# The last output block of the down projection moved into the else part of a runtime branch, with its last tile cut in two

## The chip, the cores and the metric

The kernel runs on one core of one Trainium2 chip. Times are device microseconds of one execution. The time shown for a kernel is the median of several executions; a separate execution is recorded by the hardware profiler, and that one has its own time and its own span (from the first to the last instruction of the program).

## The reference

For 2048 tokens (8 batches of 256) of 1024 features: each batch picks one of eight adapters of rank 16, and the feed-forward part works on the adapter's output, with activations rounded to FP8. The result is added to x.

```python
c      = (x @ B[adapter].T) @ A[adapter].T        # rank 16, per batch of 256 tokens
gate   = fp8(c / gate_in_scale) @ (gate_w * scales).T    # 1024 -> 2752
up     = fp8(c / up_in_scale)   @ (up_w * scales).T      # 1024 -> 2752
hidden = silu(gate) * up
out    = x + fp8(hidden / down_in_scale) @ (down_w * scales).T   # 2752 -> 1024
```

The weights are given as float32 that already hold FP8 values. `fp8` clips to 448 and rounds to float8_e4m3fn.

## The kernel before

Everything is kept transposed: features lie on the 128 partitions, tokens along the free dimension. `NH = 8` blocks of 128 features, `NI = 22` blocks of the hidden size (21 full ones and a tail of 64 rows), `NTB = 4` blocks of `TB = 512` tokens.

**Fast path.** After the adapters, `gate_up(c, t)` (L523) makes hidden block c for token block t: 16 matmuls of 128x128 weights by 512 tokens, a Silu on ScalarE (L553) and a product on VectorE that rounds to FP8 (L554). The down projection is the loop over k (L642 to L674), one k for each of the eight output blocks. For one k there are four PSUM tiles `yd`, one for each t; each takes 21 matmuls (L658) and one matmul of the 64-row tail (`tail_of`, L623). The tail of an even k is multiplied together with that of the next k, in one group of eight matmuls (L626), since two half-height matmuls run side by side. `finish` (L634) scales a tile and adds x on VectorE (L636), and starts its store from SyncE (L639); its output tile `o` has three buffers.

**The check.** The fast path takes the upper 16 bits of each float32 weight, and the chip's own FP8. That is exact only if the lower bits are zero and no rounded value reaches a limit. ScalarE therefore sums the low bits of every weight tile (`note_low_bits`, L408) and the squares of every rounded tile (`note_squares`, L415). `outside` (L604) reduces these sums with four VectorE instructions to one number for each partition, adds them over the partitions with one float32 matmul (L617), turns the sum into an integer (L619) and has every engine load it into a register (L620). It is called inside k = 7, before the last token block. If the number is positive, `general` (L67) computes everything again in three parts of each weight and with its own rounding, and overwrites the output. With this input it is never entered: the engines jump over it (L676).

**What sets the order.** A scheduler places the instructions on each engine; those wrapped in `keep_in_program_order` stay where the program has them (all of `multiply`, L423). Each engine runs its own list in order, and waits on semaphores. All weight loads and all stores of the output are issued by SyncE in one order (one queue), and the five weight buffers of the pool `w` come free when the matmuls and the low-bit sums have read them. [...]

Of the kernel before, what the change touches and what calls it, by code (L numbers as in the profile page):

```python
# [18 lines left out]
P = 128  # L19
# [47 lines left out]
def general(  # L67
# [20 lines left out]
    wpool = ctx.enter_context(tc.tile_pool(name="g_w", bufs=1))  # L88
    work = ctx.enter_context(tc.tile_pool(name="g_work", bufs=2))
    xg = acts.tile([P, NH, T], BF16, name="g_xg")  # L90
    xu = acts.tile([P, NH, T], BF16, name="g_xu")
    hid = acts.tile([P, NI, T], BF16, name="g_hid")
# [48 lines left out]
    with tc.tile_pool(name="g_lora", bufs=1) as lora:  # L141
        b_sb = lora.tile([P, NH, P], F32, name="g_b")
        nc.sync.dma_start(out=b_sb, in_=bT)
        a_sb = lora.tile([P, H], F32, name="g_a")
        nc.scalar.dma_start(out=a_sb, in_=aT)
        for t in range(NTB):
            cols = bass.ts(t, TB)
            bx = psum.tile([P, TB], F32, tag="ps", name="g_bx")
            for k in range(NH):
                xk = lora.tile([P, TB], F32, tag="xk", name="g_xk", bufs=2)  # L150
                nc.sync.dma_start(out=xk, in_=x4[t][:, k, :])
                nc.tensor.matmul(
                    bx, lhsT=b_sb[:, k, :], rhs=xk, start=(k == 0), stop=(k == NH - 1)
                )
            bm = lora.tile([P, TB], F32, tag="bm", name="g_bm")
            for j in range(TB // SEQ):
                b = t * (TB // SEQ) + j
                nc.vector.tensor_scalar(
                    bm[:, bass.ts(j, SEQ)],
                    bx[:, bass.ts(j, SEQ)],  # L160
                    mask[:, b : b + 1],
                    None,
                    ALU.mult,
                )
            for k in range(NH):
                c = psum.tile([P, TB], F32, tag="ps", name="g_c")
                nc.tensor.matmul(
                    c, lhsT=a_sb[:, bass.ts(k, P)], rhs=bm, start=True, stop=True
                )
                for to, s in ((xg, GATE_IN), (xu, UP_IN)):  # L170
                    v = work.tile([P, TB], F32, tag="v", name="g_v")
                    nc.scalar.activation(v, c, AF.Copy, scale=inv[:, s : s + 1])
                    quantize(to[:, k, cols], v, P)

    for c in range(NI):
        n = rows_of(c)
        w = wpool.tile([P, 2 * NH * P], F32, tag="w", name="g_wgu")
        at = c * 2 * NH * P
        nc.sync.dma_start(out=w[:, : 2 * NH * n], in_=w_gu[:, at : at + 2 * NH * n])
        w = w[:, : 2 * NH * n]  # L180

        order = "p (j k n) -> p j k n" if n == P else "p (k j n) -> p j k n"
        ws = [
            high(part).rearrange(order, j=2, k=NH) for part in three_parts(w)
        ]
        for t in range(NTB):
            cols = bass.ts(t, TB)
            ps = []
            for j, x in enumerate((xg, xu)):
                y = psum.tile([P, TB], F32, tag="ps", name=f"g_y{j}")[:n]  # L190
                terms = [(k, part) for part in ws for k in range(NH)]
                for i, (k, part) in enumerate(terms):
                    nc.tensor.matmul(
                        y,
                        lhsT=part[:, j, k, :],
                        rhs=x[:, k, cols],
                        start=(i == 0),
                        stop=(i == len(terms) - 1),
                    )
                ps.append(y)  # L200
# [11 lines left out]
            quantize(hid[:n, c, cols], v, n)  # L212

    for k in range(NH):
        ys = [psum.tile([P, TB], F32, tag="ps", name=f"g_yd{t}") for t in range(NTB)]
        for half in range(2):
            first = half * HALF
            full = HALF - half
            w = wpool.tile([P, 2 * NH * P], F32, tag="w", name="g_wd")
            w = w[:, : HALF * P].rearrange("p (c n) -> p c n", n=P)  # L220
            nc.sync.dma_start(out=w[:, :full], in_=w_d[k][:, first : first + full, :])
            if half:
                nc.sync.dma_start(out=w[:TAIL, full], in_=w_d_tail[:, k, :])
            terms = [(part, i) for part in three_parts(w[:, :full]) for i in range(full)]
            for t in range(NTB):
                for i, (part, at) in enumerate(terms):
                    nc.tensor.matmul(
                        ys[t],
                        lhsT=high(part[:, at, :]),
                        rhs=hid[:, first + at, bass.ts(t, TB)],  # L230
                        start=(half == 0 and i == 0),
                        stop=False,
                    )
        tail = three_parts(w[:TAIL, HALF - 1])
        for t in range(NTB):
            cols = bass.ts(t, TB)
            for i, part in enumerate(tail):
                nc.tensor.matmul(
                    ys[t],
                    lhsT=high(part),  # L240
                    rhs=hid[:TAIL, NI - 1, cols],
# [7 lines left out]
                o, in0=ys[t], scalar=down_s, in1=xr, op0=ALU.mult, op1=ALU.add  # L249
            )  # L250
            nc.gpsimd.dma_start(out=outT[bass.ts(k, P), cols], in_=o)
# [3 lines left out]
def adaln_ffn(  # L255
# [24 lines left out]
    nc.vector.memset(zeros, 0.0)  # L280

# [7 lines left out]

    with ExitStack() as fast:  # L290
        acts = fast.enter_context(tc.tile_pool(name="acts", bufs=1))
        lora = fast.enter_context(tc.tile_pool(name="lora", bufs=1))
        wpool = fast.enter_context(tc.tile_pool(name="w", bufs=5))
# [4 lines left out]
        xg = [acts.tile([P, NH, TB], FP8, name=f"xg{t}") for t in range(NTB)]  # L298
        hid = [acts.tile([P, T], FP8, name=f"hid{c}") for c in range(NI - 1)]


        hid_tail = acts.tile([P, 2, TB], BF16, name="hid_tail")
# [96 lines left out]


        wt = acts.tile([P, NH, P], F32, name="w_dt")
# [202 lines left out]
        def outside():  # L604

            nc.vector.tensor_scalar(ok[:, :NLOW], lows, 0.0, None, ALU.is_le)
            nc.vector.tensor_scalar(
                ok[:, NLOW : NLOW + NSQ], squares, SAME_MAX**2, None, ALU.is_lt
            )
            least = const.tile([P, 1], F32, name="least")  # L610
            nc.vector.tensor_reduce(least, ok, AX.X, ALU.min)
            found = const.tile([P, 1], F32, name="found")
            nc.vector.tensor_scalar(found, least, 0.5, None, ALU.is_lt)
            ones = const.tile([P, 1], F32, name="ones")
            nc.vector.memset(ones, 1.0)
            count = psum.tile([P, TB], F32, tag="ps", name="count")
            nc.tensor.matmul(count[:1, :1], lhsT=found, rhs=ones, start=True, stop=True)  # L617
            count_i = const.tile([1, 1], I32, name="count_i")
            nc.vector.tensor_copy(count_i, count[:1, :1])  # L619
            return nc.values_load(count_i[0:1, 0:1], min_val=0, max_val=P)  # L620


        def tail_of(k, ys, start):  # L623

            for t in range(NTB):
                nc.tensor.matmul(  # L626
                    ys[t],
                    lhsT=high(wt[half_of(t), k, :]),
                    rhs=hid_tail[half_of(t), t // 2],
# [4 lines left out]
        def finish(k, t, y):  # L634
            o = work.tile([P, TB], F32, tag="o", name="o")
            nc.vector.scalar_tensor_tensor(  # L636
                o, in0=y, scalar=down_s, in1=xs[t][:, k, :], op0=ALU.mult, op1=ALU.add
            )
            nc.sync.dma_start(out=outT[bass.ts(k, P), bass.ts(t, TB)], in_=o)  # L639


        for k in range(NH):  # L642
            ws = []
            for half in range(2):
# [4 lines left out]
                ws += [w[:, i, :] for i in range(n)]  # L649
            if k == 0:  # L650
                note_squares(hid_tail, P, NSQ - 1)
                note_low_bits(wt, P, NLOW - 1)
            first = k % 2 == 0
            if first:
                ys = [psum.tile([P, TB], F32, tag="ps", name=f"yd{t}") for t in range(NTB)]
            for t in range(NTB):
                for c in range(NI - 1):
                    nc.tensor.matmul(  # L658
                        ys[t],
                        lhsT=high(ws[c]),  # L660
                        rhs=hid[c][:, bass.ts(t, TB)],
                        start=(first and c == 0),
                        stop=(not first and c == NI - 2),
                    )
                if not first:
                    finish(k, t, ys[t])
                if k == NH - 1 and t == NTB - 2:
                    others = outside()
            if first:
                tail_of(k, ys, start=False)  # L670
                for t in range(NTB):
                    finish(k, t, ys[t])
                ys = [psum.tile([P, TB], F32, tag="ps", name=f"yd{t}") for t in range(NTB)]
                tail_of(k + 1, ys, start=True)  # L674

    with tc.If(others > 0):  # L676
# [3 lines left out]
        )  # L680

# [74 lines left out]
```

## Time and profile before

| | before |
|---|---|
| median of 3 runs | 481.49 us (481.45 to 482.52) |
| the profiled execution: its own time | 480.64 us |
| its span, first to last instruction | 478.8 us |
| TensorE busy | 471.0 us, 98% of the span |
| VectorE busy | 105.4 us, 22% |
| ScalarE busy | 192.6 us, 40% |
| granted TensorE clock | 0.998 of full speed |
| down projection, 8 blocks of k (L626, L658) | 323.2 to 472.8 us |
| after the last matmul to the end of the span | 6.0 us |

How to read it: PE is TensorE's matmuls and PEld its weight loads, which overlap them; DVE is VectorE, ACT ScalarE, POOL GpSimd, SP SyncE. A `q` behind an engine's name is its sequencer: instructions that take no time on the engine itself (a branch, a register load, a semaphore, the issue of a DMA). In the chain of work each piece was released by the one before it. A group of instructions shows how many there were, their busy time in us and the mean ns of one. DMA landing is the time from the issue of a transfer until its completion is signalled.

### The profile page before, as it was taken

The page shows a single profiled execution, that of the slowest core. Times are in us where ns is not written, and L with a number is a line of the kernel's source. Part 1 is how long each engine was busy: PE and PEld are TensorE (multiplying, and loading weights), DVE is VectorE, ACT ScalarE, POOL GpSimd, SP SyncE. Part 2 cuts the span into 40 slices and gives each one's busy share as a digit, 9 for nine tenths or more (in the row PEclk, how much of TensorE's full clock was granted, in tenths as well). Part 3 has the DMA queues.
Part 4 walks back from the last instruction along what each step waited for, and adds up shares of the span by engine and source line. Part 5 has one row for each costly group of instructions (what it writes and reads, how often), then busy time and mean ns, then how long its engine had stood idle before and what let it go on. Part 6 is the DMA issues. An engine that isn't in the chain of part 4 may idle for free.

```text
span 478.8 us, 6069 instructions
## 1 busy us (share of the span) xinstructions
PE 471.0 (98%) x2550; PEld 220.4 (46%) x2550; DVE 105.4 (22%) x165; ACT 192.6 (40%) x249; POOL 0.2 (0%) x4
## 2 busy tenths in 40 slices
PE   8999999999999999999999999999999999999995
PEld 7455444444444444444444444444444444444442
DVE  1342522121212121212122221232120120111021
ACT  1331519995555645443345555459112112011000
POOL 0000000000000000000000000000000000000000
PEclk9999999999999999999999999999999999999999
DMA  8998004422222112222220011111524435342031
GB/s 293 418 344 247 1 0 178 175 89 88 88 89 88 57 40 81 88 88 89 88 89 22 23 60 57 60 55 62 169 101 137 127 121 159 80 168 100 0 133 51
DMA packets 13317, 52.67 MB, mean 110 GB/s; under 512 B 1570, under 2 KB 2594, under 8 KB 9826
## 3 DMA queue, kind: packets, MB, share of 16 engines
q1 hardware_dynamic: 13136, 52.14, 31.9%
q8 instruction: 22, 0.36, 0.3%
q14 instruction: 13, 0.11, 0.1%
q10 hardware_dynamic: 146, 0.07, 0.0%
HBM read 43.81 MB, written 8.39 MB: 109 GB/s over the span
## 4 chain that ended last, share of the span: by engine, by line
PE 97%; DMA 2%; SPq 0%; DVE 0%; issue 0%
PE y L424 62%; PE yd L658 30%; PE c L424 2%; PE bx L424 1%; DMA x<-x 1%; PE yd L626 1%; DMA ids_i<-ids 0%; DVE o L636 0%; SPq L317 0%; PE warm L424 0%; SPq L320 0%; SPq L331 0%; PE count L617 0%
## 5 line engine op out<-in xcount | busy, mean ns | idle before, releaser
L424 PE MATMUL y<-xg,w_gu 128*128 128x512 fp8e4 x1376 | 298.2, 379 | 0.1
L424 PEld LDWEIGHTS <-w_gu 128*128 128x128 bf16 x1376 | 134.1, 98 | 162.8 <-issue 1.5
L658 PE MATMUL yd<-hid,w_d 128*128 128x512 fp8e4 x672 | 146.1, 379 | 0.0
L553 ACT ACTIVATE g<-y,gate_s 128x512 f32<-128x512 f32 (+1 forms) x88 | 59.8, 681 | 136.4 <-PE y L424 136.4
L554 DVE SCALAR_TENSOR_TENSOR hid<-y,up_by_down,g 128x512 fp8e4<-128x512 f32 x84 | 63.1, 751 | 219.0 <-PE y L424 152.0
L658 PEld LDWEIGHTS <-w_d 128*128 128x128 bf16 x672 | 65.4, 98 | 79.8 <-issue 1.7
L410 ACT ACTIVATE junk<-w_d 128x1408 bf16<-128x1408 uint16 (+1 forms) x16 | 21.2, 1324 | 88.6 <-DMA w_d<-w_d 88.4
L636 DVE SCALAR_TENSOR_TENSOR o<-yd,down_s,x 128x512 f32<-128x512 f32 x32 | 23.0, 748 | 118.1 <-PE yd L626 62.3
L410 ACT ACTIVATE junk<-w_gu 128x2048 bf16<-128x2048 uint16 (+1 forms) x22 | 41.0, 1863 | 0.1
L417 ACT ACTIVATE junk<-hid 128x2048 bf16<-128x2048 fp8e4 x21 | 40.0, 1905 | 0.4
L417 ACT ACTIVATE junk<-xg 128x2048 bf16<-128x2048 fp8e4 x8 | 15.2, 1904 | 0.2
L471 ACT ACTIVATE xg<-c,inv 128x512 fp8e4<-128x512 f32 x16 | 9.7, 688 | 8.4 <-PE c L424 8.4
L469 DVE TENSOR_SCALAR xg<-c,inv 128x512 fp8e4<-128x512 f32 x16 | 10.9, 745 | 2.6 <-PE c L424 2.6
L424 PE MATMUL warm<-zeros 128*128 128x128 bf16 x84 | 7.6, 270 | 1.0 <-DVE zeros L280 1.0
L424 PEld LDWEIGHTS <-zeros 128*128 128x128 bf16 x84 | 7.0, 126 | 1.6 <-DVE zeros L280 1.0
L424 PE MATMUL bx<-x,b 128*32 128x128 f32 x128 | 4.3, 276 | 0.7 <-DMA x<-x 0.7
L458 ACT COPY bm<-bx 64x128 f32<-64x128 f32 x2 | 0.5, 260 | 10.4 <-DMA w_gu<-w_gu 8.3
L424 PE MATMUL c<-bm,a 16*128 16x128 f32 x128 | 4.3, 278 | 0.0
L410 ACT ACTIVATION_READ_ACCUMULATOR junk<-w_gu 128x1 f32 x22 | 4.2, 190 | 0.0
L626 PE MATMUL yd<-hid_tail,w_dt 64*128 64x512 bf16 x32 | 4.2, 379 | 0.0
L424 PEld LDWEIGHTS c<-bm,a 16*128 16x128 f32 x128 | 3.9, 186 | 0.5 <-ACT bm L462 0.4
L424 PE MATMUL c<-bm,a_four 16*128 16x256 f32 x64 | 4.1, 389 | 0.0
(42 smaller groups left out, 37.1 us busy)
## 6 DMA issues: line engine op xcount, KB each, us to landing
w_gu<-w_gu SPq DMA_DIRECT2D x20, 1024.0 KB, 4.8
outT<-o SPq DMA_DIRECT2D x32, 256.0 KB, 2.5
x<-x SPq DMA_DIRECT2D x7, 1024.0 KB, 10.9
w_d<-w_d SPq DMA_DIRECT2D x8, 704.0 KB, 5.1
w_d<-w_d SPq DMA_DIRECT2D x8, 640.0 KB, 3.9
w_gu<-w_gu SPq DMA_DIRECT2D x3, 512.0 KB, 5.2
x<-x SPq DMA_DIRECT2D x2, 512.0 KB, 5.2
a<-a SPq DMA_DIRECT2D x4, 128.0 KB, 8.9
```

Source lines behind the costliest of these rows:

```text
L410: nc.scalar.activation(junk_like(w), low(w), AF.Copy, accum_out=lows[:rows, column : column + 1])
L417: nc.scalar.activation(junk_like(q), q, AF.Square, accum_out=squares[:rows, column : column + 1])
L424: tc.keep_in_program_order(nc.tensor.matmul(*args, **kwargs))
L458: tc.keep_in_program_order(copy(bm[j][rows, 0], bx[j][rows]))
L469: nc.vector.tensor_scalar(to, c, scale, None, ALU.mult, saturate=False)
L471: nc.scalar.activation(to, c, AF.Copy, scale=scale, saturate=False)
L553: nc.scalar.activation(g[rows], gates, AF.Silu, scale=gate_s[: gates.shape[0]])
L554: nc.vector.scalar_tensor_tensor(to, in0=ups, scalar=up_by_down[rows], in1=g[rows], op0=ALU.mult, op1=ALU.mult, saturate=False,)
L626: nc.tensor.matmul(ys[t], lhsT=high(wt[half_of(t), k, :]), rhs=hid_tail[half_of(t), t // 2], start=start, stop=not start,)
L636: nc.vector.scalar_tensor_tensor(o, in0=y, scalar=down_s, in1=xs[t][:, k, :], op0=ALU.mult, op1=ALU.add)
L658: nc.tensor.matmul(ys[t], lhsT=high(ws[c]), rhs=hid[c][:, bass.ts(t, TB)], start=(first and c == 0), stop=(not first and c == NI - 2),)
```

## The change

- The loop over k ends at k = 6. The last output block, k = 7, stands in the else part of the branch on the number of rows found (`tc.If` with the label "general", and its `Else`). The branch is taken by all engines ahead of k = 7, no longer behind it.
- The number is computed in k = 6, behind t = 1: the four VectorE instructions in their given order, then one bfloat16 matmul with a 128x128 matrix of ones (in place of a float32 one with a single column), and a copy by ScalarE. All engines load it behind the matmuls of k = 6 and before its `finish`.
- The block of t = 3 of k = 6 is wrapped in a block of its own with a prefetch hint for TensorE: the branch "general" is likely taken.
- The weights of k = 7 and its slice of x (four transfers of 256 KB, into the space of the two FP8 tiles `xg0` and `xg1`) are loaded ahead of the branch.
- The last token block of k = 7 is cut: 384 tokens, then 128 tokens. The tail rows of the piece of 128 are multiplied with `wt_odd`, a full-height bfloat16 copy of the tail weights whose other half is zero.
- `general` works on 512 tokens at a time, in a loop over t, so that its tiles fit beside the weights and tiles that are now kept. It stores from ScalarE's queue. It stays unentered.
- The tile pools of the weights, outputs, `hid` and two of the `xg` move out of the fast part's scope. All of `finish` is kept in program order.

In the order of instructions that the scheduler makes, the matmuls of k = 6, t = 3 stand behind the first matmul of t = 2, ahead of its other twenty; the prefetch hint stands in front of them.

```diff
         def outside():
-            nc.vector.tensor_scalar(ok[:, :NLOW], lows, 0.0, None, ALU.is_le)
...
-            found = const.tile([P, 1], F32, name="found")
-            ones = const.tile([P, 1], F32, name="ones")
-            nc.vector.memset(ones, 1.0)
+            found = const.tile([P, 1], BF16, name="found")
+            held(nc.vector.tensor_scalar(found, least, 0.5, None, ALU.is_lt))
             count = psum.tile([P, TB], F32, tag="ps", name="count")
-            nc.tensor.matmul(count[:1, :1], lhsT=found, rhs=ones, start=True, stop=True)
+            multiply(count[:, :1], lhsT=ones, rhs=found, start=True, stop=True)
             count_i = const.tile([1, 1], I32, name="count_i")
-            nc.vector.tensor_copy(count_i, count[:1, :1])
-            return nc.values_load(count_i[0:1, 0:1], min_val=0, max_val=P)
+            held(nc.scalar.copy(count_i, count[:1, :1]))
+            return count_i
...
-        for k in range(NH):
+        for k in range(NH - 1):
+            ws = load_down(k)
             if k == 0:
                 note_squares(hid_tail, P, NSQ - 1)
                 note_low_bits(wt, P, NLOW - 1)
+                odd = half_of(NTB - 1)
+                tc.keep_in_program_order(
+                    nc.scalar.copy(wt_odd[odd], high(wt[odd, NH - 1, :]))
+                )
+            last = k == NH - 2
+            if last:
+                ws_last = load_down(k + 1)
+                x_last = []
+                for t in range(NTB):
+                    x = xg[t // 2].rearrange("p k n -> p (k n)").bitcast(F32)
+                    x_last.append(x[:, bass.ts(t % 2, TB)])
+                    nc.sync.dma_start(out=x_last[t], in_=x4[t][:, k + 1, :])
             first = k % 2 == 0
             if first:
-                ys = [psum.tile([P, TB], F32, tag="ps", name=f"yd{t}") for t in range(NTB)]
-            for t in range(NTB):
...
+                tiles = down_tiles(NTB)
+            for t, cols, y in tiles:
+                with ExitStack() as hinted:
+                    if last and t == NTB - 1:
+                        hinted.enter_context(tc.block())
+                        tc.mark_branch_hint_location(
+                            "general", "LikelyTaken", [mybir.EngineType.PE]
+                        )
+                    times_down(ws, t, cols, y, start=first, stop=not first)
                 if not first:
-                    finish(k, t, ys[t])
-                if k == NH - 1 and t == NTB - 2:
-                    others = outside()
+                    finish(k, t, cols, y, xs[t][:, k, :])
+                if last and t == 1:
+                    count_i = outside()
             if first:
-                tail_of(k, ys, start=False)
...
+                rest_of(k, tiles, start=False)
+                if last:
+                    others = nc.values_load(count_i[0:1, 0:1], min_val=0, max_val=P)
+                for t, cols, y in tiles:
+                    finish(k, t, cols, y, xs[t][:, k, :])
+                if not last:
+                    tiles = down_tiles(NTB)
+                    rest_of(k + 1, tiles, start=True)
 
-    with tc.If(others > 0):
+    with tc.If(others > 0, label="general") as found_others:
         general(
             tc, psum, x4, aT, bT, w_gu, w_d, w_d_tail, outT, ids,
             inv=inv, gate_s=gate_s, up_by_down=up_by_down, down_s=down_s,
         )
+    with found_others.Else():
+        k = NH - 1
+        cut = TB - P
+        tiles = down_tiles(NTB - 1)
+        tiles.append(
+            (NTB - 1, slice(0, cut), psum.tile([P, cut], F32, tag="ps", name="yd"))
+        )
+        rest_of(k, tiles, start=True)
+        for t, cols, y in tiles:
+            times_down(ws_last, t, cols, y, start=False, stop=True)
+            finish(k, t, cols, y, x_last[t][:, cols])
+        t, cols = NTB - 1, slice(cut, TB)
+        y = psum.tile([P, P], F32, tag="ps", name="yd")
+        multiply(y, lhsT=wt_odd, rhs=hid_tail[:, t // 2, cols], start=True, stop=False)
+        times_down(ws_last, t, cols, y, start=False, stop=True)
+        finish(k, t, cols, y, x_last[t][:, cols])
```

`rest_of`, `times_down` and `down_tiles` are the loops of `tail_of`, L657 to L664 and L655, with the columns as an argument; `finish` takes its columns and its x as arguments.

## The prediction

> **What bounds the kernel now.** First the page: which engine fills the span, and what the chain that ended last is made of.
>
> ```profile
> span 478.8 us, 6069 instructions
> PE 471.0 (98%) x2550; PEld 220.4 (46%) x2550; DVE 105.4 (22%) x165; ACT 192.6 (40%) x249; POOL 0.2 (0%) x4
> PE 97%; DMA 2%; SPq 0%; DVE 0%; issue 0%
> ```
>
> TensorE is the bound from end to end, and the change removes no large matmul. So only the two ends of the span can pay, and the change leaves the start alone. Next the chain in order of time for the last stretch (start us, us, what):
>
> ```profile
> 465.88 2.16 PE yd L658 x10
> 468.04 0.12 PE count L617 x2
> 468.16 4.66 PE yd L658 x21
> 472.82 0.02 issue
> 472.84 0.75 DVE o L636
> ```
>
> The chain stops at VectorE's last `o`, at 473.6. The span goes on to 478.8, 6.0 us behind the last matmul. This is what fills it. In the view by line of the branch and of the number's load, each row has the engine, the instruction, its ns (min/median/max) and its start:
>
> ```profile
> L620 PEldq TENSOR_LOAD <-count_i x1: 492/492/492, 468.9 to 468.9; - x1
> ...
> L676 PEldq COMPARE_BRANCH  x1: 3782/3782/3782, 469.5 to 469.5; - x1
> ...
> L676 DVEq COMPARE_BRANCH  x1: 72/72/72, 473.5 to 473.5; - x1
> ...
> L676 DVEq EVENT_SEMAPHORE  x1: 21/21/21, 476.4 to 476.4; - x1
> ```
>
> TensorE's sequencer stood at its branch for 3.78 us; VectorE's is through its branch at 473.55 and runs its next instruction at 476.4, 2.8 us later. Both are loads of instructions at a far target. And the store of the last tile, in the view of `outT`, took 3.1 us from its issue at 473.6 to landing, where the one before it took 2.2. The DMA view of 473.4 to 477.0 (40 slices of 0.09 us) tells why:
>
> ```profile
> GB/s 0 0 0 0 0 0 0 182 0 0 0 159 364 341 319 319 319 341 341 182 137 0 46 46 23 46 0 46 23 23 23 0 0 0 0 0 0 0 0 91
> ...
> q8 instruction: 1, 0.02, 2.0%
> ```
>
> The store runs at over 300 GB/s from 474.4 to 475.2, and then drips at one 2 KB packet a slice (23 GB/s) until 476.2: one DMA engine is late. It was held by the 16 KB instruction packet of q8 (the burst of 182 in the eighth slice, 474.1), which TensorE's sequencer asked for behind its branch. Landing at 476.7 and 2.1 us of semaphores and barriers close the span. So the end is: last matmul 472.8, VectorE 0.75, store 3.1, closing 2.1.
>
> **The change part by part.**
>
> *The cut of the last tile, TensorE.* The full-clock pace of 128-column pairs (weight load and matmul) is shown by the warm-up; the timeline gives one group of it, start, length and count:
>
> ```profile
> 5.77 1.24 PE L424 MATMUL warm<-zeros 128*128 128x128 bf16 x19
> ```
>
> Nineteen in 1.24 us; the last one lasts 0.219 (the minimum of that tile's view), so (1.24 - 0.219)/18 = 0.057 us a pair. At 512 columns the chain has 36.37 us for 168, 0.216 each. On the line between them 384 columns cost 0.163. Before: 21 x 0.216 = 4.54. After: 21 x 0.163 + 22 x 0.057 (one more, `wt_odd`) = 3.42 + 1.25 = 4.67, so +0.13. The run-out of the last matmul is the same (0.379 - 0.216 = 0.163 at 512, 0.219 - 0.057 = 0.162 at 128). [...] The trace shows 57, but with one weight tile of zeros loaded over and over. For real weights no row exists; the record of one load is 98 ns for both (`w_d`, and zeros at full clock), so I take 57. [...] if each load took its whole 98, 0.9.
>
> *The count.* Two passes in float32 cost 0.12 us in the chain; one bfloat16 pass at 128 rows is taken as one pair of 57 ns: -0.06. It moves to about 444.3, the end of t = 1 of k = 6. What it needs is there: the last low-bit sum ended at 438.6 and the VectorE instructions that use it at 439.2, 5 us earlier. If they came late, TensorE itself would stand at the count; nothing is queued ahead of them on VectorE but the stores' `o` of k = 5, done at 436.0.
>
> *The branch ahead of k = 7.* Every engine now crosses it with work behind it.
> TensorE: 0.49 for the load plus 3.78 at the branch is 4.3 us in which its sequencer sends nothing. What covers it is the work already queued: before, the sequencer loaded the number at 468.9 with matmuls in the queue up to 472.8, so at least 3.9 us. The prefetch hint stands some 45 pairs ahead, about 9.7 us, longer than the whole load. With it the branch should take what VectorE's took when it stalled for nothing, under 0.1. I take 0. Without the hint and with the shown cover it is 0.4; with no cover at all 3.8 to 4.3. [...]
> VectorE: its four `o` of k = 6 end at 457.8 as now (the fourth waits for an output buffer), then the branch, 2.9 us: next `o` at 460.7 where 459.0 was possible. It is late by 1.7, but the tile after it is only ready at 463.5. No matmul needs its PSUM tile back by then[...]. SyncE behind it: its branch follows the store at 457.8, so it is back by some 461. ScalarE and GpSimd have nothing in the else part. Cost 0, with 2 us to spare on VectorE.
>
> *Loads of x and weights.* Four transfers of 256 KB stand in SyncE's queue behind the second half of k = 1's weights (issued at 316.4 plus) and ahead of k = 2's first (323.3). They wait for the last matmuls of gate_up on t = 0 and 1, before 320, so k = 2's load isn't held; and it is needed only at 360. The DMA engines are 22% busy between 52 and 323 us, by the view of stretches. If they were late, that weight load would be next, with 36 us of cover. The weights of k = 7 go out as now, at 433.1. Cost 0.
>
> *The end.* VectorE's last operation shrinks from 512 to 128 columns:
>
> ```profile
> L636 DVE SCALAR_TENSOR_TENSOR o<-yd,down_s,x 128x512 f32<-128x512 f32 x32 | 23.0, 748 | 118.1 <-PE yd L626 62.3 <-PE yd L658 42.2 <-DMA outT<-o 13.5
> ...
> L458 DVE COPY bm<-bx 64x128 f32<-64x128 f32 x2 | 0.6, 283 | 7.7 <-PE bx L424 7.7
> L499 DVE COPY bm<-bx 128x256 f32<-128x256 f32 x1 | 0.4, 424 | 4.9 <-PE bx L424 4.9
> ```
>
> 128 more columns of PSUM cost 424 - 283 = 141 ns, so 0.75 - 3 x 0.141 = 0.33: -0.42. The piece of 384 (0.61 by the same line) starts 1.25 us earlier and is done.
> The last store is 64 KB instead of 256 KB, and no far branch comes just before it, so no instruction load should sit in its way. Undisturbed, 256 KB land in 2.1 (the minimum of `outT`), of which some 0.8 is transfer (ten slices above). A quarter of that leaves 1.5; nothing saved by size leaves 2.1. [...] I take 1.7: -1.4. [...]
> VectorE's own late return from the branch (476.4) goes too, so landing alone decides. One short branch at the end of the else part: +0.05.
>
> *Sum.* TensorE +0.13 - 0.06, VectorE -0.42, store -1.4, branch +0.05: -1.7 us. Span 478.8 to 477.1; the profiled execution's own time, 480.64 with 1.84 around the span, to 478.9. The median, 481.49, is 0.85 above that execution; the same difference makes 479.8, 0.35% less.
>
> **The rivals.** 0.3%, 1.44 us, is about what a measurement of this kernel can tell from no change: below 480.05 is faster, above 482.93 slower.
> *Half the gain.* [...] For it: no row has real weights at this pace, and no small store exists in the trace. Against it: equal load records, and the slices above.
> *The store still meets an instruction load.* Some engine's next 16 KB or 8 KB fall due at the end: the store keeps 1 us of delay, 480.8. Against it: engines fetch soon after they enter the else part, at 448 to 462.
> *TensorE stands at the branch (slower).* Place: between k = 6's tail matmuls at 454 and those of k = 7. If the 3.78 us is not covered, or if it was the sequencer waiting for the array to drain (it ended at 473.3, 0.5 behind the last matmul), the array stands idle. Price up to 3.8: -1.7 + 3.8 = +2.1, 483.6. From 1.7 us of visible stall the gain is gone, from 3.15 it is slower by over 0.3%. Against it: VectorE's branch ended at 473.55 while its `o` ran until 473.6, so a branch doesn't drain an engine there; and the hint. For it: TensorE's own branch has no second row.
>
> **How the numbers follow.** Forecast 0.56 (479.8, own range 479.2 to 480.05); half the gain 0.25; store still late 0.07; TensorE at the branch 0.12, of which 0.08 over 482.93. Some of the two middle cases falls under 480.05 and some of the first above it, and I let these cancel. Faster 0.56, same 0.34 (with small branch stalls, and other losses that I can't name taken from it), slower 0.10. The range 479.0 to 482.0 takes in the forecast, the two middle cases and half of the branch case.
>
> **What would show it.** The last matmul at 472.8 to 473.0 in the chain, with no idle time at 454; count as one short matmul near 444; TensorE's branch under 0.5 us; the last `o` of 128 columns at 0.33; the last store landing in 1.5 to 2.1 with no slow drip behind it; 2.1 from landing to the end. The prediction is wrong if 128-column pairs stand over 70 ns apart, if TensorE is idle between k = 6 and k = 7, or if the last landing stays at 3.

## The result, and the profile after

The changed kernel takes 477.94 us (median of 6, 477.53 to 479.29) where the kernel before takes 481.47 (6 runs): a ratio of 0.9927, 95% interval 0.9912 to 0.9942. Run once more beside the later experiments it took 478.41 against 481.36, ratio 0.9946 (0.9931 to 0.9961). So it is 3.0 to 3.5 us faster. The prediction had 1.7, and its range ended at 479.0. The direction was right, and the gain about twice what was expected.

The page of the changed kernel, the lines that answer to those shown of before:

```profile
span 476.3 us, 6119 instructions
...
PE 470.4 (99%) x2571; PEld 221.1 (46%) x2571; DVE 105.4 (22%) x164; ACT 192.8 (40%) x251; POOL 0.5 (0%) x6
...
PE 93%; DMA 5%; SPq 1%; issue 0%; DVE 0%
```

TensorE is still the bound. (The chain has more DMA because in this execution it runs back through a later load at the start.) The chain in order of time from 466 us on:

```profile
465.87 7.46 PE yd L438 x56
473.33 0.03 issue
473.35 0.35 DVE o L653
```

The last matmul ends at 473.3, no earlier than before (472.8); what follows it is 2.9 us instead of 6.0. The two executions don't start alike: the first down matmul stands at 323.67 here and at 323.06 before, 0.6 later, since the loads of x at the start took longer (the first in the chain 6.79 us instead of 6.29). From there to the last matmul's end it is 149.64 against 149.74. So all of the gain but 0.1 lies behind the last matmul:

| us | before | after | difference | predicted |
|---|---|---|---|---|
| first down matmul to last matmul's end | 149.74 | 149.64 | -0.10 | +0.07 |
| VectorE's last `o` | 0.75 | 0.35 | -0.40 | -0.42 |
| last store, issue to landing | 3.09 | 1.64 | -1.45 | -1.4 |
| last landing to the end of the span | 2.07 | 0.88 | -1.19 | +0.05 |
| sum | | | -3.14 | -1.7 |

-3.14 and the later start, +0.61, make the difference of the spans, 478.8 to 476.3. One execution's start differs from another's by about that much (the same kernel's runs lie 1 to 2 us apart), so the medians, 3.5 and 3.0 apart, are the better measure of the whole, and the segments the better measure of the parts. (The parts of the end of the span are taken from the times of single records, so some have one digit more than the rows shown.)

The last tile, in the timeline of TensorE (start us, us, what), and its VectorE operations in the groups by form:

```profile
471.27 0.81 PE L438 MATMUL yd<-hid,w_d 128*128 128x384 fp8e4 x4
471.92 0.22 PE L438 MATMUL yd<-hid_tail,w_dt_odd 128*128 128x128 bf16 x1
471.98 1.34 PE L438 MATMUL yd<-hid,w_d 128*128 128x128 fp8e4 x21
```

```profile
L653 DVE SCALAR_TENSOR_TENSOR o<-yd,down_s,xg 128x384 f32<-128x384 f32 x1 | 0.6, 618 | 2.7 <-PE yd L438 2.7
...
L653 DVE SCALAR_TENSOR_TENSOR o<-yd,down_s,xg 128x128 f32<-128x128 f32 x1 | 0.4, 352 | 0.6 <-PE yd L438 0.6
```

(1.34 - 0.219)/20 = 0.056 us for each pair of a new weight tile and 128 columns: real weights keep the pace of the zeros that the prediction took it from.

The branch, by line (ns and start us of each):

```profile
L730 PEldq COMPARE_BRANCH  x1: 388/388/388, 451.4 to 451.4; - x1
L730 DVEq COMPARE_BRANCH  x1: 72/72/72, 457.5 to 457.5; - x1
L730 SPq COMPARE_BRANCH  x1: 53/53/53, 458.7 to 458.7; - x1
```

TensorE's took 0.39 us instead of 3.78, and its matmuls run on without a gap. And the end, in the DMA view of 473.4 to 476.0 (40 slices of 0.065 us), with the only instruction load in it and the time of the last store to landing:

```profile
GB/s 0 0 0 236 307 354 378 378 378 378 378 190 48 0 0 0 0 32 165 299 268 189 55 0 0 0 0 0 0 0 0 126 0 0 0 0 0 0 0 0
...
q14 instruction: 1, 0.01, 1.1%
...
outT<-o SPq DMA_DIRECT2D x1, 64.0 KB, 1.6
```

First the store of 384 columns, then that of 128, in six slices and with no drip; the one instruction load (126, at 475.4) comes when the store has landed. The same two rows in the prediction's view of before:

```profile
q14 instruction: 3, 0.02, 2.2%
...
outT<-o SPq DMA_DIRECT2D x1, 256.0 KB, 3.1
```

The completion signals say more: a store has sixteen of them in the trace, as many as the page counts DMA engines. Before, fourteen of the last store's came by 475.81, and the last two at 476.26 and 476.71. In the changed kernel all sixteen of the last store came between 475.17 and 475.37.

### The profile page after: what moved, and what is told of

Read it like the earlier page. It is cut to its first block, busy times and chain, and to the rows that moved or that the text cites. A ratio compares the mean times of both kernels' runs of the same rounds, so it can differ in the third digit from the quotient of the medians.

```text
span 476.3 us, 6119 instructions
## 1 busy us (share of the span) xinstructions
PE 470.4 (99%) x2571; PEld 221.1 (46%) x2571; DVE 105.4 (22%) x164; ACT 192.8 (40%) x251; POOL 0.5 (0%) x6
## 4 chain that ended last, share of the span: by engine, by line
PE 93%; DMA 5%; SPq 1%; issue 0%; DVE 0%
PE y L438 60%; PE yd L438 31%; DMA x<-x 5%; PE c L438 1%; PE bx L438 1%; SPq L337 0%; DMA ids_i<-ids 0%; SPq L348 0%; SPq L334 0%; DVE o L653 0%; PE count L438 0%
## 5 line engine op out<-in xcount | busy, mean ns | idle before, releaser
L438 PE MATMUL yd<-hid,w_d 128*128 128x512 fp8e4 (+2 forms) x693 | 146.0, 373 | 0.0
L438 PEld LDWEIGHTS <-w_d 128*128 128x128 bf16 x693 | 66.6, 98 | 79.0 <-issue 1.7
L653 DVE SCALAR_TENSOR_TENSOR o<-yd,down_s,x 128x512 f32<-128x512 f32 x28 | 20.0, 747 | 107.5 <-PE yd L438 93.8
L653 DVE SCALAR_TENSOR_TENSOR o<-yd,down_s,xg 128x512 f32<-128x512 f32 (+2 forms) x5 | 3.2, 645 | 12.2 <-PE yd L438 12.2
L438 PEld LDWEIGHTS bx<-x,b 128*32 128x32 f32 x128 | 3.3, 109 | 3.0 <-DMA x<-x 1.9
L438 PE MATMUL yd<-hid_tail,w_dt 64*128 64x512 bf16 (+1 forms) x32 | 4.2, 377 | 0.0
```

The lines of the kernel that those rows point to most:

```text
L438: tc.keep_in_program_order(nc.tensor.matmul(*args, **kwargs))
L653: nc.vector.scalar_tensor_tensor(o, in0=y, scalar=down_s, in1=x, op0=ALU.mult, op1=ALU.add)
```

## The experiments

Two questions were open: why the end of the span shrank by 1.2 us that nothing was expected of, and how much each part of the change gives by itself. Each kernel below leaves the computation whole.

| kernel | last matmul to end of span, us | last store | last landing to end | ratio to before, 95% |
|---|---|---|---|---|
| before | 5.98 | 3.09 | 2.07 | 1 |
| before, last semaphore of the list | 6.22 | 3.28 | 2.12 | 0.9996 (0.9983 to 1.0010) |
| before, hint | 5.62 | 2.73 | 2.07 | 0.9985 (0.9973 to 0.9998) |
| before, general's stores on ScalarE's queue | 5.55 | 2.97 | 1.76 | 0.9995 (0.9983 to 1.0008) |
| before, cut | 5.75 | 2.87 | 2.46 | 0.9995 (0.9985 to 1.0005) |
| before, cut, hints, ScalarE's queue | 5.41 | 2.87 | 2.13 | 0.9986 (0.9977 to 0.9995) |
| changed | 2.94 | 1.64 | 0.88 | 0.9927 (0.9912 to 0.9942) |
| changed, again | 2.94 | 1.64 | 0.88 | 0.9946 (0.9931 to 0.9961) |
| changed, third semaphore of the list | 3.29 | 1.69 | 1.19 | 0.9935 (0.9918 to 0.9953) |
| changed, no cut | 4.03 | 2.26 | 0.96 | 0.9960 (0.9946 to 0.9974) |
| changed, no hint | 2.95 | 1.65 | 0.88 | 0.9951 (0.9933 to 0.9969) |
| changed, general's stores on GpSimd's queue | 3.01 | 1.65 | 0.95 | 0.9953 (0.9939 to 0.9968) |
| changed, a far branch behind the end | 5.53 | 2.30 | 2.81 | 1.0016 (1.0006 to 1.0025) |

**The place of the last store's semaphore.** Behind the last store SyncE works off a list of waits, among them one for each of eight DMA semaphores (the eight entries of L676 in the trace of before), in a fixed order. In the kernel before, the last store signals the third of them, in the changed one the eighth. Tiny loads shift that:

```diff
                     nc.sync.dma_start(out=wt[half_of(t)], in_=w_d_tail)
+                for i in range(3):      # changed kernel; 5 in the kernel before
+                    tiny = const.tile([1, NB], I32, name=f"tiny{i}")
+                    nc.sync.dma_start(out=tiny, in_=ids)
```

> The changed kernel with three tiny loads more (32 bytes each, beside the loads of w_dt, mid-kernel), which do nothing but shift which of the eight DMA semaphores the last store signals: the third of them, as in the kernel before, instead of the eighth. Theory 1: SyncE's closing list waits for these semaphores in their fixed order, and the changed kernel was lucky that its last store has the last place in that list, so that the list is worked off while the store is under way. Then this kernel is 1.0 to 1.2 us slower than the changed one (about 479.0), all of it between the last landing and the end (0.9 becomes 2.0). Theory 2: the closing got shorter because no branch stands near the end any more. Then nothing changes (477.9).

> The kernel before with five tiny loads more (32 bytes each, beside the loads of w_dt), which shift the last store's semaphore from the third to the eighth and last of the closing list. Nothing else is changed: branch at the end, no cut, the store still beside the instruction load (3.1 us). Theory 1 (the order of the list): 1.0 to 1.2 us faster than the kernel before, about 480.4, all of it behind the last landing. Theory 2 (the closing is short only without a branch near it): no change, 481.5.

Theory 1 missed in both: the changed kernel with the third semaphore took 478.06, the kernel before with the eighth 481.38 against 481.44. The place alone is not worth 1.1 us. The traces say what it is worth. The closing instructions of SyncE in the kernel before, from the last landing on (the line of the branch, then that of the program's end):

```profile
L676 SPq EVENT_SEMAPHORE  x6: 17/17/17, 476.7 to 477.1; - x6
```

```profile
L751 SPq EVENT_SEMAPHORE  x12: 28/28/28, 477.2 to 477.8; - x12
```

18 entries from 476.73 to 477.87, 0.065 us each, all behind the landing at 476.71. And in the changed kernel the program's end in the two stretches around the landing at 475.37, 473.9 to 475.36 and 475.37 to 475.6:

```profile
L822 SPq EVENT_SEMAPHORE  x7: 17/28/28, 474.4 to 475.1; - x7
```

```profile
L822 SPq DRAIN  x2: 7/10/13, 475.5 to 475.5; - x2
L822 SPq EVENT_SEMAPHORE  x1: 27/27/27, 475.4 to 475.4; - x1
```

Seven entries while the store is under way, one behind it. So the cost is the number of entries behind the last landing: 17 fewer are 1.12 of the 1.19 us. The other 0.07 lies in the barrier of all engines behind the list, 0.73 us instead of 0.81. Moving the semaphore in the changed kernel put five more entries behind the store's landing at 475.06:

```profile
L825 SPq EVENT_SEMAPHORE  x6: 28/28/28, 475.1 to 475.4; - x6
```

Last landing to end is 1.19 instead of 0.88, and times can't tell 0.3 us from nothing. In the kernel before, all eight DMA semaphores are waited for ahead of the second part of the list; the eighth place saves five entries, 0.3 us, and leaves thirteen. In that run this doesn't show (2.12 instead of 2.07), since the list stands still for some 0.4 us near its end; why is not known.

**The length of the list.** Four of the twelve pairs are gone from the changed kernel's list. `general` stores from ScalarE's queue there. So the kernel before was given that edit alone.

```diff
-            nc.gpsimd.dma_start(out=outT[bass.ts(k, P), cols], in_=o)
+            nc.scalar.dma_start(out=outT[bass.ts(k, P), cols], in_=o)
```

> The kernel before with a single edit in the part that is never entered: general stores from ScalarE's queue, not GpSimd's. In the trace of before SyncE's closing list has 12 pairs of semaphores at 0.065 us, four of which are gone from the changed kernel's list. If those four belong to GpSimd's stores: four pairs fewer, all behind the last landing, so closing 2.07 becomes 1.8, the kernel 0.2 to 0.3 us faster, 481.2. If unentered code costs nothing: no change in the list.

The list is four pairs shorter, and last landing to end is 1.76 instead of 2.07: -0.32 (0.24 in four entries, the rest in the barrier), for an edit of code that never runs. The times don't tell it from nothing (481.03 against 481.38, interval of the ratio across 1). The same edit the other way in the changed kernel:

> The changed kernel with general's stores on GpSimd's queue again, as in the kernel before (never entered). This brought four pairs of semaphores into the closing list, 0.3 us in the trace of the kernel before. Here the list is worked off while the last store is under way, up to the pair with that store's own semaphore. If the four stand ahead of it, they cost nothing: closing 0.88 and 477.9. If the list's length counts by itself: 0.3 us slower, 478.2, closing 1.2.

The profile of that run has twelve entries in the list at the program's end, from 474.6 on, and again only the one with the store's own semaphore behind the landing:

```profile
L822 SPq EVENT_SEMAPHORE  x12: 17/28/28, 474.6 to 475.7; - x12
L822 SPq DRAIN  x2: 7/10/12, 475.8 to 475.8; - x2
```

0.95 from landing to end: the four entries cost nothing where the store hides them, and the 0.07 lies in the barrier again. Its median, 478.90 against 478.41, lies within the spread of the two. Beside it the changed kernel was run again as it is:

> The changed kernel itself once more, beside the two others, for its profile and times on the same chip: 477.9, 2.9 us from the last matmul to the end, store 1.6 to 1.7, closing 0.9.

It took 478.41 us, with the same 2.94, 1.64 and 0.88 in its trace.

**The hint at the old place.** To see whether TensorE's instruction load is what delays the last store. So that the hint keeps its place, the down matmuls and that of the count are kept in program order here, and the number is loaded behind the loop.

```diff
+                with ExitStack() as hinted:
+                    if k == NH - 1 and t == 1:
+                        hinted.enter_context(tc.block())
+                        tc.mark_branch_hint_location(
+                            "general", "LikelyTaken", [mybir.EngineType.PE])
...
-    with tc.If(others > 0):
+    with tc.If(others > 0, label="general"):
```

> The kernel before with the branch where it was, behind k = 7, but a prefetch hint for TensorE in front of t = 1 of k = 7 (in a block of its own), so that its instruction load is over long before the last store. No cut. If that load is what holds one DMA engine back at the end: the last store lands in 2.1 to 2.3 us instead of 3.1 to 3.3, with no drip, and the kernel is 0.7 to 1.0 us faster, 480.6. If the drip has another cause, the store stays at 3.1 and the time at 481.4.

TensorE's branch took 0.40 us and its load was over before the store, yet the store still took 2.7 us, between the two expectations, and the ratio is 0.9985. Its DMA view from 473.9 to 477.5 (slices of 0.09 us):

```profile
GB/s 0 0 0 0 0 0 0 0 0 114 387 341 387 341 364 341 364 182 23 46 114 23 23 23 23 0 0 0 0 0 0 0 0 0 0 0 0 91 0 0
...
q14 instruction: 3, 0.02, 2.5%
...
outT<-o SPq DMA_DIRECT2D x1, 256.0 KB, 2.7
```

No load of q8 is left in the window, but the drip is still there, shorter. It follows an 8 KB packet of q14 at 474.85, 0.69 us long; by its time, 1.0 us behind VectorE's branch, this is VectorE's load. Eight packets of 2 KB are delivered last, until 476.2: one DMA engine's sixteenth of the store. Fifteen completion signals came by 476.17, the last at 476.68. So the prediction named the right kind of cause and only one of its sources: before, two DMA engines were late, here one is. In these two runs the store landed with the last of its signals, at 476.71 and 476.68, and in each a DMA engine was late behind a load in the store's window: TensorE's in the kernel before (16 KB, 1.16 us), VectorE's here (8 KB, 0.69 us). (The trace doesn't name the DMA engine of a packet; that the late one is the one with the load is read from the times.) From the last matmul to the end this run gains 0.36 us; the time shows less of it, since a tail matmul leaves its group and TensorE's stream is 0.21 us longer (149.96).

**The cut at the old place, then everything at the old place.** The cut as in the changed kernel, with the branch behind k = 7; and the cut together with hints for TensorE and VectorE and general's stores on ScalarE's queue.

```diff
+                if k == NH - 1 and t == NTB - 1:
+                    c0 = TB - P
+                    y = psum.tile([P, P], F32, tag="ps", name="yd_cut")
+                    nc.tensor.matmul(y, lhsT=wt_odd, rhs=hid_tail[:, t // 2, c0:], ...)
+                    ...
+                    finish(k, t, y, c0)
```

> The kernel before with the cut alone (384 and 128 with wt_odd), the branch at the end. TensorE +0.1, VectorE -0.4. The queue of TensorE now holds short matmuls when its sequencer comes to the branch, so the branch starts about 0.9 us before the last matmul and its instruction load runs from 473.5 to 474.7: the small store lands in about 2 us. TensorE and VectorE come back from their branches at 476.4 to 476.5, which then ends last. Together 0.9 to 1.4 us faster, 480.3. If the cut alone gave its full price (VectorE 0.4, store 1.4), it would be 1.8 faster, 479.7.

> The kernel before with the branch at the end, and all that can be had there: the cut, hints for TensorE and VectorE in front of t = 1 of k = 7, general's stores on ScalarE's queue. Theory 1: what the move ahead of k = 7 gives is the store's free way (had by the hint), no return from a far branch at the end (had by the hints), and a closing list that is worked off while the store is under way (not had: here all eight DMA semaphores are waited for first). Then the last store lands in 1.7, the closing is 1.6 to 1.9, and the kernel is 2.0 to 2.5 us faster than before, 479.2. Theory 2, the move itself gives something else as well: under 1.5 us, 480 and more. Theory 3, the move gives nothing of its own: 3.5 us, 477.9.

The cut alone gives nothing that can be measured (ratio 0.9995), where 0.9 to 1.4 us were expected. VectorE is 0.4 us shorter, but the store of 64 KB takes 2.87 us with two completion signals late, little less than one of 256 KB; and the closing is 0.39 longer, since SyncE's list stands still for 0.35 us at one place, for a reason that is not known. Everything together gives 0.5 us (480.88). (The end gains 0.57 in the trace, and TensorE's stream, 150.06, takes back 0.32.) Of the three theories only the second (under 1.5 us) has such a number; its reason, that the move itself gives something else as well, is tested by the next run. Theory 1 fails at the store, 2.87 instead of 1.7, and theory 3 at the time. Why shows in its branch rows (ns and start us):

```profile
L709 PEldq COMPARE_BRANCH  x1: 398/398/398, 472.8 to 472.8; - x1
...
L709 DVEq COMPARE_BRANCH  x1: 84/84/84, 474.2 to 474.2; - x1
L709 DVEq EVENT_SEMAPHORE  x1: 21/21/21, 477.1 to 477.1; - x1
```

TensorE's hint worked, but with short matmuls in the queue its sequencer only reaches the branch at 472.8, and the next 16 KB of q8 are loaded behind it at 474.4, in 1.1 us of the store's window: fifteen completion signals came by 475.35, the last at 476.58. VectorE's hint changed nothing: it went on 2.9 us after its branch, as in the kernel before (473.5 to 476.4). So at the end of the program these means didn't make a far branch free.

**A far branch put back.** The opposite test: the changed kernel with the same condition asked once more behind its last store.

```diff
         finish(k, t, cols, y, x_last[t][:, cols])
+        with tc.If(others > 0):
+            general(...)
```

> The changed kernel, with a second far branch put back at its very end: behind the last store of the else part the same condition is asked again, and general stands behind it once more (never entered). The number is in the registers already, nothing is loaded for it. Theory 1: it is not that k = 7 was moved that pays, but that no far branch stands at the end any more. Then the last store meets instruction loads again (2.6 to 3.0 us instead of 1.64), all eight DMA semaphores are waited for before the closing list, and the end of the span is 5.0 to 5.5 us behind the last matmul instead of 2.9: 2.1 to 2.6 us slower, 480.0 to 480.5. Theory 2: the gain lies elsewhere, for instance in TensorE's stream or in k = 7's place: under 0.5 us slower, 478.4 or less.

482.24 us, slower than the kernel before (ratio 1.0016), 3.8 more than the changed kernel beside it; even theory 1 had no more than 2.6. The part that it speaks of came as it says, except for the store. From the last matmul to the end it is 5.53 us instead of 2.94: the store 2.30 (below the 2.6 to 3.0 expected, and 0.32 of its growth is a longer issue), then 2.81 until the end. SyncE's rows say why (ns and start us):

```profile
L752 SPq EVENT_SEMAPHORE  x8: 17/17/17, 477.9 to 478.4; - x8
...
L752 SPq COMPARE_BRANCH  x1: 45/45/45, 475.4 to 475.4; - x1
```

It comes back from its own branch only at 477.9, 0.9 us behind the landing, with the whole list of 16 entries still to do. TensorE's stream from the first down matmul to the last is the same, 149.64. So k = 7's new place gives nothing by itself; that no engine crosses a far branch at the end gives 2.6 us of span here. (That is more than the 1.95 which lie between the kernel before and the changed kernel without the cut, since this one also loses what the cut gains. The other 1.2 us of its time lie outside the segment, and their cause is open: 0.6 between the span and the execution's own time, 482.17 against 479.8, and 0.6 in its start.)

**No cut.** What the cut gives once the branch is out of the way:

```diff
-        tiles = down_tiles(NTB - 1)
-        tiles.append((NTB - 1, slice(0, cut), psum.tile([P, cut], F32, ...)))
+        tiles = down_tiles(NTB)
...
-        t, cols = NTB - 1, slice(cut, TB)
...
```

> The changed kernel without the cut: the last tile is one piece of 512. Branch ahead of k = 7, hint and all else stay. By the parts of the prediction: TensorE -0.1, VectorE +0.4, store of 256 KB 2.1 to 2.2 instead of 1.64 (no instruction load beside it): +0.5, and its semaphore is now next to last in the closing list: +0.07. Together +0.9, about 478.8. If it was the cut that kept the last store clear of the instruction load, the store takes 3.1 again and the sum is +1.9, 479.8.

479.27, 1.3 above the first and 0.9 above the second measurement of the changed kernel. In the trace the end is 1.09 us longer: VectorE 0.40, the store 0.62 (2.26 and undisturbed), the list 0.07. TensorE is 0.11 shorter. That is the +0.9 expected, part by part. The cut is worth 1.0 us here, and at the old place nothing that the times show.

**No hint.** The lines that give TensorE's branch its hint are left out; everything else stays.

```diff
-            tc.mark_branch_hint_location(
-                "general", "LikelyTaken", [mybir.EngineType.PE])
```

> The changed kernel without the prefetch hint; the block around t = 3 of k = 6 stays. In the changed kernel's trace TensorE's sequencer comes to the number's load at 450.8 and the array gets through what was sent until then at 454.4: 3.5 us of cover. A branch of 3.8 us as in the kernel before resumes at 455.3. Theory 1: TensorE stands 0.8 to 1.0 us at the branch, 478.8. Theory 2: the queue holds more than that, or the branch finds its target without a hint: no idle time, 477.9.

479.19. TensorE's timeline (start us, us, what) shows it standing between the tails of k = 6 and those of k = 7:

```profile
454.01 0.61 PE L438 MATMUL yd<-hid_tail,w_dt 64*128 64x512 bf16 x4
455.05 0.60 PE L438 MATMUL yd<-hid_tail,w_dt 64*128 64x512 bf16 x4 [0.43 <-issue]
```

(Tails are half-height and run two at a time: the first four start within 0.23 us, in two pairs 3 to 4 ns apart.) Its branch took 3.47 us from 451.5, and the way from the first down matmul to the last is 150.25 instead of 149.64: 0.6 us lost. The first theory holds in the trace, a little below its size; the median, 0.8 to 1.3 above the two of the changed kernel, lies a little above it. So the rival in which TensorE stands at the branch was real, and the hint is what kept it away.

No run takes back the count's new form, the new form of `general` or the moved pools by itself. TensorE's stream, 149.64 against 149.74, leaves them little to have changed there.

## Why the prediction was wrong

*The end of the span* is the step that failed. The working has "Landing at 476.7 and 2.1 us of semaphores and barriers close the span", and carries the 2.1 unchanged into the sum, with 0.05 for one more branch. It is 0.88. This term, -1.19 where +0.05 was put, is nearly all of the gap between -1.7 and -3.1. The view from which the branch's rows were taken has another one:

```profile
L676 SPq EVENT_SEMAPHORE  x8: 17/17/17, 474.5 to 477.1; - x8
```

Only one of these eight waits for the last store; those behind it, and the list, only stand in line, at 0.065 us an entry. The prediction took the whole as a fixed close and did not ask which entries wait for the store. The experiments show two of the parts, by segments and near the limit of what can be told: 0.3 for the four pairs of GpSimd's queue (at the old place; at the new one 0.07) and 0.3 for the five entries behind the third semaphore. The rest, the second part of the list, was not changed alone: it stood behind the landing and now runs while the store is under way, and it is behind the landing again (2.81) where a far branch is put back at the end.

*The last store* held: 1.7 was taken, 1.64 measured, between the 1.5 and the 2.1 that its working names. Its reason held in part. "one DMA engine is late" and "It was held by the 16 KB instruction packet of q8" name one of two late engines; q14's row, with three loads of 8 KB, stood in the same view. Taking q8's packet away leaves 2.7 us. Only with no engine's load in its way did the store land in 1.64 (2.26 at 256 KB). The loads that the prediction puts at 448 to 462 are in the changed kernel's trace: six of 8 KB and one of 16 KB between 446 and 462.5, and the next only at 475.5, behind the landing.

*VectorE's last operation*, 0.33 expected, is 0.35. *The cut on TensorE*, 0.057 expected for a pair, is 0.056 with real weights. The rival with half the gain, that these pairs run slower and the small store keeps 2.1, fell with it and with the 1.64. The whole cut costs TensorE 0.11, where 0.13 was put. *The count* was mis-sized: 0.06 saved was expected. From the matmul ahead of it to the one behind it, it was 0.43 us, and is 0.24 now; a plain step is 0.216. So the array's loss shrank from 0.21 to 0.03 us, 0.19 saved, and the extra 0.13 is most of the 0.17 by which TensorE's term is better than predicted. Why it cost so much is open: it was float32, in two passes, and its weights had one column (the steps to and from the 64-row weights of the tails are 0.31, too); no run took this edit alone.

*The branch ahead of k = 7* held at each engine: VectorE's next `o` started at 460.9 (460.7 expected), SyncE's next store could be prepared at 461.6 (461), TensorE lost nothing. The cover was right in kind and a little large: 3.5 us are shown, not 3.9 (without the hint 0.6 lost, where 0.4 was expected for this case). It is 17 pairs in both places; the four that are tails take less time (eight tails 0.97 us in the trace of before, 0.12 each, where a pair of 512 columns takes 0.216).

*The median.* The prediction took the profiled execution's 0.85 us to the median as fixed. That depended on single executions: the one profiled before had an early start (its first down matmul at 323.06; 323.2 to 323.6 in the profiles of the other kernels with the branch at the end), and that of the changed kernel, 478.07, lies 0.13 above its median, not below. This difference of 0.98 and the later start of 0.61 partly cancel. The end of the span alone, 1.24 beyond its term, would have made 478.6 of the predicted 479.8.

## What to carry to other kernels

The end of a kernel is a stage of its own: list every instruction between the last landing and the end of the span, and ask of each whether it waits for the last transfer or only stands behind something that does. A far branch cost more than its own stall here: instructions were loaded behind it, and a store of 64 KB that was under way at that moment landed in 2.30 to 2.87 us instead of 1.64. What paid was to cross the branch where matmuls were queued ahead (3.5 us of them), to hint it for the engine that sets the pace (0.6 us of TensorE), and to leave straight code at the end (2.6 us of span). The smaller last store paid (1.0 us) only where no instruction load stood in its window; at the old place the ratio was 0.9995.

## What the runs showed of the hardware

- An instruction load took 0.3 to 0.9 us at 8 KB and 0.9 to 1.4 at 16 KB (the traces of before and of the changed kernel). With such loads in its window a store of 64 KB took 2.30 to 2.87 us and one of 256 KB 2.73 to 3.28; undisturbed 1.64 to 1.69 and 2.1 to 2.3.
- TensorE's sequencer ran 3.5 us ahead of the array: it came to the number's load at 450.8 with 13 pairs of 512 columns and four tail pairs to go, 34 instructions. In all 13 traces it began this load with 17 pairs to go; with 128-column pairs (the kernel before with the cut) they are some 1.0 us. Without a hint that did not cover the branch of 3.47 us and the load of the number ahead of it: 0.6 us was lost. What limits it to 34 is open.
- A branch that its hint had prepared took 0.39 to 0.40 us on TensorE, without one 3.4 to 3.8. Asked for on VectorE in the same way, the hint changed nothing: 2.9 us to the next instruction. No run shows why.
- Code that is never entered took 0.3 us in the trace: the queue that its stores name adds four entries of some 0.06 us to the list at the program's end. The times can't tell this from nothing.
